# Row maxima and head sums sent round by DMA instead of TensorE transposes, with the order of the DMAs fixed

## The chip, the cores and the metric

The kernel runs on one core of one Trainium2 chip. The metric is the device time of one launch in microseconds (us). In this text PE is TensorE, DVE is VectorE, ACT is ScalarE, POOL is GpSimd, and SP is SyncE, whose queue issues nearly all DMAs of this kernel. SBUF is the on-chip memory of 128 partitions, PSUM the accumulators that TensorE writes (eight banks of 128 x 512 float32).

## The reference

The input x is 4 batches of 2048 rows of 256 float32. Attention with 16 heads of 16, then a normalized residual, then a gated feed-forward whose operands are quantized in blocks of 16 to a 4-bit grid, then a second normalized residual:

```
q, k, v = split_heads(x @ Wq.T), split_heads(x @ Wk.T), split_heads(x @ Wv.T)
attn = softmax(einsum('bhld,bhmd->bhlm', q, k) * SCALE)
x = layernorm(x + merge(einsum('bhlm,bhmd->bhld', attn, v)) @ Wo.T)
x = layernorm(x + fp4_linear(silu(fp4_linear(x, w_gate)) * fp4_linear(x, w_up), w_down))
```

`fp4_linear` scales each block of 16 values by its largest magnitude / 6, rounds to the grid 0, 0.5, 1, 1.5, 2, 3, 4, 6, and multiplies in float32.

## The kernel before

The attention is worked off in 64 steps: 4 batches x 4 blocks of 512 query rows (QB) x 4 groups of 4 heads. A step has 16 periods (NKT), one for each 128 key rows; so the main loop has 1024 periods, and 64 periods make one block of query rows. Periods are counted 0 to 15 within a step below. In a period TensorE makes, by an order written out by hand (ORDER):

- four score products `pm` (line 178, called by `maximum`) of a step ahead: 128 query rows by 512 keys, of which VectorE takes the largest of each row (`mx`, recorded at line 95, the line of the helper class InOrder);
- four score products `pe` (`exponential`) of the present step, turned the other way: 128 keys by 512 query rows, which ScalarE turns into `e` with exp (line 567);
- four products of `e` with the values into the bank `av` (`values`), two periods later. The values carry columns of ones, so that `av` holds each head's numerator and its sum of exponentials, in 16 + 16 rows a head;
- at most one *part* of other work: the projections of a later batch (`square`), the feed-forward (`wide`, `long`) or four transposes (`turn`). A period without a part has the kind `none`.

The maxima run 20 periods (LEAD) ahead of the exponentials. The negative of a row's maximum must stand in the last two of the 64 rows of each head's `q` tile (a high and a low half), opposite rows of ones in `k`, so that the product `pe` is already less the maximum. `max_rows` does that, from period 11 of a step on: VectorE's reduction `nm`, two GpSimd operations that split it into `nh` (lines 537, 538), a part `pn` of four transposes in period 13, a copy `nr` by ScalarE (line 549), and four DMAs from `nr` into the `q` tiles (line 554). The first `pe` that reads them stands in period 0 of the next step of exponentials.

`normalize` divides a finished step, from period 1 of the next step on: ScalarE copies the bank to `av_sb` (line 588), a part `pa` of four transposes turns it in period 3, VectorE takes the reciprocals `rd` of the sums and makes two products `oq`. After every second step a part `pr` of four transposes turns `oq` back, and ScalarE copies it to `oT` (line 615), which the residual's products `py` read.

Work of the feed-forward on VectorE and GpSimd is put into a list of due times (`later`, `take_due`): at most one entry is run in a period, after the last maximum, and none in a period in which `normalize` has set `clock["busy"]`. Quantizing (`fp4`) is such a chain: `amax`, then `sc` and `rs` on VectorE and `xn` on GpSimd, then the mask `m` on VectorE and four GpSimd operations (lines 242 to 245). The generator of the feed-forward goes on only when a number of periods has passed since the last entry.

TensorE's and VectorE's instructions stay in the order of the program (`keep_in_program_order`). Those of ScalarE, GpSimd and the DMAs on SP are placed by a scheduler. SP works in order: a DMA that waits holds all behind it. q, k and v go through DRAM (`qx`, `kx`, `vx`) and are loaded again step by step by `loads`.

Of the kernel before, what the change touches and what calls it, by code (L numbers as in the profile page):

```python
# [35 lines left out]
F32 = mybir.dt.float32  # L36
# [71 lines left out]
def block_kernel(  # L108
# [47 lines left out]
    def later(periods, step, rest=0):  # L156
# [2 lines left out]
        due.append((clock["now"] + periods, step, state))  # L159
        return lambda: state["done"] is not None and clock["now"] >= state["done"] + rest  # L160

    def take_due(most=1):
# [61 lines left out]
    def fp4(pool, t, tag, gain=1.0):  # L224

        p, nb, _ = t.shape
        amax = pool.tile([p, nb], F32, tag="amax" + tag, name="amax")
        vector.tensor_reduce(amax, t, AX.X, ALU.max, apply_absolute_value=True)
        sc = pool.tile([p, nb], F32, tag="sc" + tag, name="sc")
        xn = pool.tile([p, nb, FB], F32, tag="xn" + tag, name="xn", bufs=3 if tag else 2)  # L230

        def scaled():
            vector.tensor_scalar(sc, amax, gain / 6.0, 1e-12, ALU.mult, ALU.max)
            rs = pool.tile([p, nb], F32, tag="rs" + tag, name="rs")
            vector.reciprocal(rs, sc)
            nc.gpsimd.tensor_scalar(rs, rs, gain * TIES_DOWN, 1.0, ALU.mult, ALU.mult)
            nc.gpsimd.tensor_tensor(xn, t, rs.unsqueeze(2).to_broadcast([p, nb, FB]), ALU.mult)
# [9 lines left out]
        later(1, scaled)  # L247
        return xn, later(3, rounded, 4 if tag == "" else 3)

    def fp4_at_once(pool, t, tag, gain=1.0):  # L250

# [36 lines left out]

    kx = [[dram.tile([R, NC, L], F32, tag=f"kx{i}{c}", name=f"kx{i}{c}") for c in range(KC)] for i in range(2)]
    qx = [[dram.tile([R, NC, QB], F32, tag=f"qx{i}{c}", name=f"qx{i}{c}") for c in range(KC)] for i in range(6)]  # L290
    vx = [dram.tile([NG, P, NKT, NP * 3 * DH], F32, tag=f"vx{i}", name=f"vx{i}") for i in range(2)]

    p1 = ctx.enter_context(tc.tile_pool(name="p1", bufs=1))
# [3 lines left out]
    def load_x(b, tb):  # L297

        rows = slice(tb * QB, (tb + 1) * QB)
        if b == 0 and tb >= 2:  # L300
            xb_of[b, tb] = p1.tile([P, QT, D], F32, tag="x1", name="xb", bufs=2)
        else:
            xb_of[b, tb] = p2.tile([P, QT, D], F32, tag="xb", name="xb")
        nc.sync.dma_start(xb_of[b, tb], x[b, rows, :].rearrange("(t p) d -> p t d", p=P))


    loaded = {}
# [40 lines left out]
    def prepare():  # L348
# [82 lines left out]
    def project(b, tb, what):  # L431
# [14 lines left out]
        def q_or_k(name, c):  # L446
# [9 lines left out]
                was_read("pq")  # L456
                yield LEAST

            for i, half in enumerate((hi, lo, hi, lo) if name == "k" else (hi, hi, lo, lo)):
                d = min(DH, RM - i * DH)  # L460
                nc.sync.dma_start(
                    dst[i * DH : i * DH + d].rearrange("r h n -> (r h) n"), half[: d * NC, :].bitcast(F32)
                )
            projected.add((b, tb, name + str(c)))

        def values_of():
            for t in range(QT):
                v = vt[(tb * 2 + t // 2) % 4]
                pv = psum("pv")
                yield product(pv[:, :D], [(xT[:, kc, t * P : (t + 1) * P], wvT[:, kc, :]) for kc in range(KC)])  # L470
                src = pv[:, :D].rearrange("p (g i j d) -> p g i j d", g=NG, i=NP, j=2)
                for j in range(2):
                    nc.scalar.copy(v[:, :, t % 2, :, 2 * j * DH : (2 * j + 1) * DH], src[:, :, :, j, :])
                if t % 2:
                    t0 = tb * QT + t - 1
                    nc.sync.dma_start(
                        vx[b % 2][:, :, t0 : t0 + 2, :].rearrange("g p t c -> p g (t c)"),
                        v.rearrange("p g t i c -> p g (t i c)"),
                    )
                if t == QT - 1:  # L480
                    projected.add((b, tb, "v"))
                was_read("pv")
                yield LEAST

# [6 lines left out]
    def load_q(s):  # L491
        b, qb, g = steps[s]
        for i in range(NP):
            c, h = divmod(g * HG + i * 2, NC)
            q = p1.tile([P, QB], F32R, tag="q", name="q", bufs=3 * NP)
            for j in range(2):
                nc.sync.dma_start(
                    q[R * j : R * j + RM, :].bitcast(F32), qx[(b * NQB + qb) % len(qx)][c][:RM, h + j, :]
                )
            q_sb[s, i] = q  # L500

    def load_k(s, kb):
        b, qb, g = steps[s]
        for i in range(NP):
            c, h = divmod(g * HG + i * 2, NC)
            k = p1.tile([P, QB], F32R, tag="k", name="k", bufs=16)
            for j in range(2):
                nc.sync.dma_start(
                    k[R * j : R * j + R, :].bitcast(F32), kx[b % 2][c][:, h + j, kb * QB : (kb + 1) * QB]
                )  # L510
            k_sb[s, i, kb] = k

    def load_v(s):
        b, qb, g = steps[s]
        assert all((b, tb, "v") in projected for tb in range(NQB))
        v_sb[s] = p1.tile([P, NKT, NP * 3 * DH], F32, tag="v", name="v", bufs=2)
        nc.sync.dma_start(v_sb[s], vx[b % 2][g])

    def maximum(m, h):

        (s, n), (i, j) = divmod(m, NKT), divmod(h, 2)
        if s not in mx_sb:
            mx_sb[s] = p2.tile([P, QT, HG, NQB], F32, tag="mx", name="mx")
# [5 lines left out]
        vector.tensor_reduce(mx_sb[s][:, t, h : h + 1, kb], pm, AX.X, ALU.max)  # L529
        banks_m.append(bank)  # L530

    def max_rows(s):

        nm = p2.tile([P, QT, HG], F32, tag="nm", name="nm")
        vector.tensor_reduce(nm, mx_sb.pop(s), AX.X, ALU.max, negate=True)
        nh = p2.tile([P, QT, HG, 2], F32R, tag="nh", name="nh")
        nc.gpsimd.tensor_scalar(nh[:, :, :, 0], nm, 1.0, 1.0, ALU.mult, ALU.mult)
        nc.gpsimd.tensor_tensor(nh[:, :, :, 1], nm, nh[:, :, :, 0].bitcast(F32), ALU.subtract)
        yield 0
        yield 0  # L540
        pn = psum("pn")
        yield turn(
            [
                (pn[: 2 * HG, t * P : (t + 1) * P], nh[:, t].rearrange("p h c -> p (h c)").bitcast(F32))
                for t in range(QT)
            ]
        )
        nr = p2.tile([2 * HG, QB], F32R, tag="nr", name="nr", bufs=1)
        nc.scalar.copy(nr, pn[: 2 * HG, :])
        was_read("pn")  # L550
        for i in range(NP):
            for j in range(2):
                h = 2 * i + j
                nc.sync.dma_start(
                    q_sb[s, i][R * j + RM : R * j + R, :].bitcast(F32), nr[2 * h : 2 * h + 2, :].bitcast(F32)
                )
        yield LEAST

    def exponential(n, h):

# [19 lines left out]
                stop=(kt == NKT - 1),  # L580
            )

    oTs, oq_of = {}, {}

    def normalize(s):

        av_sb = p2.tile([P, QB], F32, tag="av_sb", name="av_sb", bufs=1)
        nc.scalar.copy(av_sb, av_ps.pop(s))
# [7 lines left out]
        vector.reciprocal(rd, pairs[:, :, :, 1:3, 0])  # L596
        clock["busy"] = True
        if s % 2 == 0:
            oq_of[s // 2] = p2.tile([P, QT, P], F32, tag="oq", name="oq", bufs=1)
# [115 lines left out]
    def feed_forward(b, qb, between):  # L715
        rows = slice(qb * QB, (qb + 1) * QB)
        x1 = p1.tile([P, QT, D], F32, tag="x1", name="x1", bufs=2)
        nc.sync.dma_start(x1, x[b, rows, :].rearrange("(t p) d -> p t d", p=P))
        if between is not None:
            load_x(*between)  # L720
        yield 0
# [24 lines left out]
        def out_rows(t):  # L746
            at = slice(qb * QB + t * P, qb * QB + (t + 2) * P)
            store = out[b, at, :].rearrange("(t p) d -> p t d", p=P)
            layer_norm(x1, t, 2, lambda: nc.sync.dma_start(store, x1[:, t : t + 2, :]))

        yield from gate(0)
        yield from gate(1)
# [218 lines left out]
    def loads(n):  # L971
# [25 lines left out]

    for n in range(-LEAD, N + LAG):
        m = n + LEAD
        loads(n)  # L1000
        if n == N - NKT:
            x1_last = load_last(*steps[-1][:2])
# [34 lines left out]
        if m >= N:  # L1037
            take_due(len(due))
    banks.extend([7])
    while urgent or queue or due or ready:  # L1040
        take_due(len(due))
        whole()
    feed_forward_last(*steps[-1][:2], x1_last)
# [32 lines left out]
```

## Time and profile before

| | us |
|---|---|
| median of 3 runs | 3491.27 (3488.14 to 3494.37) |
| profiled execution, span from the first to the last instruction | 3493.0 |
| TensorE busy | 3395.2 (97%) |
| VectorE busy | 2921.7 (84%) |
| ScalarE busy | 2627.0 (75%) |
| GpSimd busy | 1506.2 (43%) |
| 4096 maxima `mx` on VectorE | 2599.8, 682 ns each |
| transposes `pn`, `pa`, `pr` on TensorE (256, 256, 128) | 38.5, 42.1, 21.0 |
| copies `nr`, `oT` on ScalarE (64, 32) | 36.4, 18.9 |
| `oq`, `rd` on VectorE (128, 64) | 31.3, 15.8 |
| `nh`, two forms, on GpSimd (64 each) | 14.9, 14.3 |

For the profiled execution no time but its span is given, so the span stands for it; the granted TensorE clock has a mean of 0.989 in it. A line of a group reads: line, engine, operation, output <- inputs, shapes, count, then busy time in us and the mean of one in ns, then how long the engine stood idle before it and what ended that. A line of the timeline reads: start and length in us, engine, line, operation, output <- inputs, how many in a row, and in brackets the idle time before it with what ended it. Matmuls overlap each other, so that sums of their durations say little and the distance from one period to the next says more.

### The profile page before, as it was taken

To read this page: it belongs to the slowest core of one execution; us is meant where nothing else is said; L and a number is where in the kernel's file an instruction comes from. 1 tells how busy PE (TensorE), PEld (TensorE's weight loads), DVE (VectorE), ACT (ScalarE), POOL (GpSimd) and SP (SyncE) were. 2 spreads that over 40 slices of the span, in tenths; PEclk is the share of its full clock that TensorE was granted. 3 is DMA by queue.
4 is the path that set the end of the run, shared out by engine and by line. 5 is a ranking of instruction groups with operands and counts; after the bars stand their busy time and mean duration, and the time that the engine had idled before them with its cause. 6 is when DMAs were issued, how large, how long until landed. Compare 5 with 4: busy or idle time off the path is not lost.

```text
span 3493.0 us, 65842 instructions
## 1 busy us (share of the span) xinstructions
PE 3395.2 (97%) x24340; PEld 1798.9 (51%) x24340; DVE 2921.7 (84%) x5130; ACT 2627.0 (75%) x5446; POOL 1506.2 (43%) x1724
## 2 busy tenths in 40 slices
PE   7899999999999999999999999999999999999996
PEld 5444555555555555555555555555554544545444
DVE  5788888888888888888888888888888898888825
ACT  3677777877777787877778777787877778777772
POOL 1243453534435343453535336353443545344361
PEclk9999999999999999999999999999999999999998
DMA  6543323333242332333333242332332122222200
GB/s 208 177 139 114 106 82 120 91 86 108 88 120 76 119 98 63 116 100 109 92 96 102 80 120 88 106 96 76 105 88 82 58 83 69 67 77 76 71 1 12
DMA packets 190678, 328.90 MB, mean 94 GB/s; under 512 B 24344, under 2 KB 68248, under 8 KB 190360
## 3 DMA queue, kind: packets, MB, share of 16 engines
q1 hardware_dynamic: 188968, 323.39, 31.0%
q8 instruction: 195, 3.19, 0.4%
q10 hardware_dynamic: 1392, 1.31, 0.1%
q14 instruction: 123, 1.01, 0.1%
HBM read 237.04 MB, written 86.51 MB: 93 GB/s over the span
## 4 chain that ended last, share of the span: by engine, by line
PE 83%; DVE 10%; POOL 4%; DMA 2%; issue 1%; SPq 0%; ACT 0%; POOLq 0%; ACTq 0%; DVEq 0%
PE av L178 25%; PE pm L178 16%; PE pe L178 16%; DVE mx L95 7%; PE pz L178 6%; PE pg L178 4%; PE pu L178 4%; PE pq L178 3%; PE py L178 2%; PE pth L181 2%; PE pv L178 1%; POOL m L242 1%; PE pn L181 1%; PE pa L181 1%; POOL xn L243 1%; POOL xn L244 1%
## 5 line engine op out<-in xcount | busy, mean ns | idle before, releaser
L95 DVE TENSOR_REDUCE mx<-pm 128x1 f32<-128x512 f32 x4096 | 2599.8, 682 | 414.6 <-PE pm L178 240.6
L567 ACT ACTIVATE e<-pe 128x512 f32<-128x512 f32 x4096 | 2234.7, 602 | 704.3 <-PE pe L178 430.1
L178 PE MATMUL pm<-k,q 62*128 62x512 f32 x4096 | 1631.4, 446 | 45.0 <-DVE mx L95 32.6
L178 PE MATMUL pe<-q,k 64*128 64x512 f32 x4096 | 1555.9, 444 | 0.5 <-ACT read L221 0.3
L178 PE MATMUL av<-e,v 128*32 128x512 f32 x8192 | 1096.4, 607 | 4.5 <-DMA v<-vx 4.5
L178 PEld LDWEIGHTS pm<-k,q 62*128 62x128 f32 x4096 | 720.1, 186 | 721.6 <-DVE mx L95 585.8
L178 PEld LDWEIGHTS pe<-q,k 64*128 64x128 f32 x4096 | 693.6, 185 | 428.9 <-ACT e L567 357.5
L178 PE MATMUL pg<-wgT,xqT 64*128 64x352 f32 (+1 forms) x992 | 351.4, 474 | 1.8 <-ACT xqT L821 1.8
L178 PE MATMUL pu<-wuT,xqT 64*128 64x352 f32 (+1 forms) x992 | 352.5, 473 | 0.0
L178 PEld LDWEIGHTS av<-e,v 128*32 128x32 f32 x8192 | 161.7, 108 | 302.9 <-issue 269.5
L178 PE MATMUL pz<-wdT,hT 64*128 64x128 f32 (+2 forms) x2648 | 312.7, 281 | 1.5 <-ACT hT L858 1.5
L242 POOL TENSOR_SCALAR m<-m 128x704 f32<-128x704 f32 (+2 forms) x100 | 231.8, 2318 | 171.3 <-DVE m L95 169.9
L178 PEld LDWEIGHTS pz<-wdT,hT 64*128 64x128 f32 (+1 forms) x2648 | 299.7, 189 | 8.9 <-ACT hT L858 2.9
L711 POOL TENSOR_TENSOR x<-x,read 128x128 f32<-128x128 f32 x120 | 54.6, 455 | 497.1 <-ACT read L221 496.1
L675 POOL TENSOR_TENSOR a<-a,g 128x352 f32<-128x352 f32 x120 | 112.6, 938 | 344.7 <-ACT a L673 344.6
L683 POOL TENSOR_TENSOR h<-a,u 128x352 f32<-128x352 f32 x120 | 112.5, 937 | 160.7 <-ACT u L681 159.5
L178 PEld LDWEIGHTS pu<-wuT,xqT 64*128 64x128 f32 (+1 forms) x992 | 172.9, 186 | 14.5 <-issue 1.0
L178 PEld LDWEIGHTS pg<-wgT,xqT 64*128 64x128 f32 (+1 forms) x992 | 172.7, 186 | 14.5 <-ACT xqT L821 3.0
L243 POOL TENSOR_TENSOR xn<-xn,m 128x704 f32<-128x704 f32 (+2 forms) x100 | 153.8, 1538 | 6.6
L244 POOL TENSOR_TENSOR xn<-xn,m 128x704 f32<-128x704 f32 (+2 forms) x100 | 153.6, 1536 | 6.1
L245 POOL TENSOR_TENSOR xn<-xn,sc 128x704 f32<-128x704 f32 (+2 forms) x100 | 126.2, 1262 | 7.8
L455 POOL TENSOR_TENSOR klo<-read,khi 128x256 fp32r<-128x256 f32 x64 | 47.7, 747 | 188.2 <-ACT read L221 160.0
(114 smaller groups left out, 2636.5 us busy)
## 6 DMA issues: line engine op xcount, KB each, us to landing
k<-kx SPq DMA_DIRECT2D x1024, 128.0 KB
v<-vx SPq DMA_DIRECT2D x64, 768.0 KB
q<-qx SPq DMA_DIRECT2D x256, 124.0 KB
kx<-khi SPq DMA_DIRECT2D x64, 256.0 KB
qx<-qhi SPq DMA_DIRECT2D x64, 256.0 KB
vx<-vt SPq DMA_DIRECT2D x32, 384.0 KB
xb<-in_L_attn_x_dram SPq DMA_DIRECT2D x16, 512.0 KB
kx<-klo SPq DMA_DIRECT2D x32, 256.0 KB
```

The source lines that it names most:

```text
L95: return lambda *args, **kw: self.tc.keep_in_program_order(getattr(self.engine, name)(*args, **kw))
L178: tc.keep_in_program_order(nc.tensor.matmul(*args, **kw))
L181: tc.keep_in_program_order(nc.tensor.transpose(*args))
L242: nc.gpsimd.tensor_scalar(m, m, 1.0, ROUND, ALU.max, ALU.mult)
L243: nc.gpsimd.tensor_tensor(xn, xn, m, ALU.add)
L244: nc.gpsimd.tensor_tensor(xn, xn, m, ALU.subtract)
L245: nc.gpsimd.tensor_tensor(xn, xn, sc.unsqueeze(2).to_broadcast([p, nb, FB]), ALU.mult)
L455: nc.gpsimd.tensor_tensor(lo[:, cols], read(pq), hi[:, cols].bitcast(F32), ALU.subtract)
L567: nc.scalar.activation(e, pe, AF.Exp, scale=SCALE)
L675: nc.gpsimd.tensor_mul(a, a, g)
L683: nc.gpsimd.tensor_mul(h[:, cols], a, u)
L711: nc.gpsimd.tensor_add(x1[:, t, cols], x1[:, t, cols], read(pz))
```

## The change

The maxima are split by VectorE itself (a copy and a subtraction into `nh`), and one VectorE transpose of 32 x 32 squares makes `nt`. One DMA stores `nt` to a DRAM tile `mr`, and four DMAs load it from there into the rows of the `q` tiles. The part `pn` and the copy `nr` are gone.

In all steps but the last two, `normalize` makes no transposes: two DMAs gather the rows of sums out of `av_sb` into `ends` (128 x 16), three DMAs move the numerators into `num`, VectorE takes the reciprocal `rd`, one DMA stores it to a DRAM tile `sr`, one DMA loads it back, repeated over 16 rows a head, into `den`, and after every second step one GpSimd product of `num` and `den` makes `oT`. The last two steps keep the old way (`normalize_last`).

Within the main loop the DMAs that go through a new helper `dma` (all but those of the weights) stay in the order of the program. Stores of projections, values and output rows are put into the program 2 or 3 periods later than their data (`after`, `send_waiting`). The loads of v move from period 3 to 5 of a step, those of k and q from periods 0, 4, 8, 12 to 1, 5, 9, 13. The preparation of the weights waits until the piece before has been scaled (`taken`).

```diff
+    def dma(out, in_):
+        i = nc.sync.dma_start(out, in_)
+        if pinned["on"]:
+            tc.keep_in_program_order(i)
+
+    def after(periods, send):
+
+        if pinned["on"]:
+            waiting.append((clock["now"] + periods, send))
+        else:
+            send()
...
         for piece, after in zip(pieces, pieces[1:] + [None]):
+            while not q[1].taken():
+                yield LEAST
...
+            after(3, stores)
...
-        nm = p2.tile([P, QT, HG], F32, tag="nm", name="nm")
+        nm = p2.tile([P, HG, QT], F32, tag="nm", name="nm")
         vector.tensor_reduce(nm, mx_sb.pop(s), AX.X, ALU.max, negate=True)
-        nh = p2.tile([P, QT, HG, 2], F32R, tag="nh", name="nh")
-        nc.gpsimd.tensor_scalar(nh[:, :, :, 0], nm, 1.0, 1.0, ALU.mult, ALU.mult)
-        nc.gpsimd.tensor_tensor(nh[:, :, :, 1], nm, nh[:, :, :, 0].bitcast(F32), ALU.subtract)
         yield 0
+        nh = p2.tile([P, HG, 2, QT], F32, tag="nh", name="nh")
+        vector.tensor_copy(nh[:, :, 0, :].bitcast(F32R), nm)
+        vector.tensor_tensor(nh[:, :, 1, :].bitcast(F32R), nm, nh[:, :, 0, :], ALU.subtract)
         yield 0
-        pn = psum("pn")
-        yield turn(
...
-        nr = p2.tile([2 * HG, QB], F32R, tag="nr", name="nr", bufs=1)
-        nc.scalar.copy(nr, pn[: 2 * HG, :])
-        was_read("pn")
+        nt = p2.tile([P, S], F32, tag="nt", name="nt")
+        vector.transpose(nt, nh.rearrange("p h c t -> p (h c t)"))
+        rows = mr[s % 2]
+        dma(rows.rearrange("r (b q) -> b r q", q=S), nt)
+        yield 0
         for i in range(NP):
             for j in range(2):
                 h = 2 * i + j
-                nc.sync.dma_start(
-                    q_sb[s, i][R * j + RM : R * j + R, :].bitcast(F32), nr[2 * h : 2 * h + 2, :].bitcast(F32)
-                )
-        yield LEAST
+                dma(
+                    q_sb[s, i][R * j + RM : R * j + R, :].bitcast(F32),
+                    rows[h * 2 * QT : (h + 1) * 2 * QT].rearrange("(c t) p -> c (t p)", c=2),
+                )
...
     def normalize(s):
+
+        if s >= len(steps) - 2:
+            yield from normalize_last(s)
+            return
+        av_sb = p2.tile([P, QB], F32, tag="av_sb", name="av_sb", bufs=1)
+        nc.scalar.copy(av_sb, av_ps.pop(s))
+        ends = p2.tile([P, QB // S], F32, tag="ends", name="ends")
+        yield 0
+        for i in range(NP):
+            dma(
+                ends[i * R : (i + 1) * R, :],
+                av_sb[i * R + DH : i * R + 3 * DH : DH, :].rearrange("j (c n) -> j c n", n=QB // S),
+            )
...
+        for src, dst, n in ((0, 0, DH), (S + DH, DH, 2 * DH), (3 * S + DH, 3 * DH, DH)):
+            dma(num[at + dst : at + dst + n, :], av_sb[src : src + n, :])
+        for _ in range(3):
+            yield 0
+        rd = p2.tile([P, QB // S], F32, tag="rd", name="rd")
+        vector.reciprocal(rd, ends)
+        clock["busy"] = True
+        yield 0
+        dma(sr[s % 2].rearrange("h (c n) -> (h c) n", n=QB // S), rd)
+        yield 0
+        yield 0
+        dma(den[at : at + R, :], sr[s % 2].unsqueeze(1).to_broadcast([HG, DH, QB]))
+        if s % 2 == 0:
+            return
+        for _ in range(5):
+            yield 0
+        oT = p1.tile([P, QB], F32, tag="oT", name="oT", bufs=3)
+        nc.gpsimd.tensor_tensor(oT, num, den, ALU.mult)
...
-        if kt == 3 and 0 <= n and s + 1 < len(steps):
+        if kt == 5 and 0 <= n and s + 1 < len(steps):
             load_v(s + 1)
-        if n > 0 and kt % QT == 0:
-            ahead, kb = divmod(n - QT + 2 * NKT, NKT)
+        if n > 0 and kt % QT == 1:
+            ahead, kb = divmod(n - 1 - QT + 2 * NKT, NKT)
...
+        pinned["on"] = 0 <= n < N
+        send_waiting()
         loads(n)
```

More of the change, by code (lines that the diff above doesn't have):

```diff
@@ L160, in later, with send_waiting @@
         return lambda: state["done"] is not None and clock["now"] >= state["done"] + rest
+    pinned = {"on": False}
+    waiting = deque()
+    def dma(out, in_):
[7 more added lines that the diff above has]
+            send()
+    def send_waiting(everything=False):
+        for _ in range(len(waiting)):
+            at, send = waiting.popleft()
+            if everything or at <= clock["now"]:
+                send()
+            else:
+                waiting.append((at, send))
     def take_due(most=1):
@@ L290, in block_kernel @@
     qx = [[dram.tile([R, NC, QB], F32, tag=f"qx{i}{c}", name=f"qx{i}{c}") for c in range(KC)] for i in range(6)]
+    mr = [dram.tile([2 * HG * QT, P], F32, tag=f"mr{i}", name=f"mr{i}") for i in range(2)]
+    sr = [dram.tile([HG, QB], F32, tag=f"sr{i}", name=f"sr{i}") for i in range(2)]
     vx = [dram.tile([NG, P, NKT, NP * 3 * DH], F32, tag=f"vx{i}", name=f"vx{i}") for i in range(2)]
@@ L475, in values_of, with store @@
                     t0 = tb * QT + t - 1
[L476 to L481, printed above, removed]
+                    def store(t=t, t0=t0, v=v):
+                        dma(
+                            vx[b % 2][:, :, t0 : t0 + 2, :].rearrange("g p t c -> p g (t c)"),
+                            v.rearrange("p g t i c -> p g (t i c)"),
+                        )
+                        if t == QT - 1:
+                            projected.add((b, tb, "v"))
+                    after(2, store)
                 was_read("pv")
@@ L522, in maximum @@
         if s not in mx_sb:
-            mx_sb[s] = p2.tile([P, QT, HG, NQB], F32, tag="mx", name="mx")
+            mx_sb[s] = p2.tile([P, HG, QT, NQB], F32, tag="mx", name="mx")
         kb, t = n // QT, n % QT
@@ L748, in out_rows @@
             store = out[b, at, :].rearrange("(t p) d -> p t d", p=P)
-            layer_norm(x1, t, 2, lambda: nc.sync.dma_start(store, x1[:, t : t + 2, :]))
+            layer_norm(x1, t, 2, lambda: after(3, lambda: dma(store, x1[:, t : t + 2, :])))
         yield from gate(0)
@@ L1039, in block_kernel @@
     banks.extend([7])
-    while urgent or queue or due or ready:
+    while urgent or queue or due or ready or waiting:
         take_due(len(due))
+        send_waiting(True)
         whole()
```

48 lines of the change are left out of this document (28 added, 20 removed).

## The prediction

> **What bounds the kernel.** I read the page first (busy shares, chain), then the groups, then the timeline and a table by stretch.
>
> ```profile
> PE 3395.2 (97%) x24340; PEld 1798.9 (51%) x24340; DVE 2921.7 (84%) x5130; ACT 2627.0 (75%) x5446; POOL 1506.2 (43%) x1724
> ...
> PE 83%; DVE 10%; POOL 4%; DMA 2%; issue 1%; SPq 0%; ACT 0%; POOLq 0%; ACTq 0%; DVEq 0%
> ```
>
> TensorE carries the chain, but VectorE's maxima are close behind. How close, the periods tell. Each starts four `av` products:
>
> ```profile
> 1758.34 1.07 PE L178 MATMUL av<-e,v 128*32 128x512 f32 x8
> 1761.08 1.07 PE L178 MATMUL av<-e,v 128*32 128x512 f32 x8
> ...
> 1766.24 0.66 PE L181 MATMUL pa<-ident,av_sb 128*128 128x128 f32 x4
> 1767.48 1.07 PE L178 MATMUL av<-e,v 128*32 128x512 f32 x8
> 1769.84 0.66 PE L181 MATMUL pr<-ident,oq 128*128 128x128 f32 x4
> 1771.10 1.07 PE L178 MATMUL av<-e,v 128*32 128x512 f32 x8
> ...
> 1774.02 1.07 PE L178 MATMUL av<-e,v 128*32 128x512 f32 x8
> ```
>
> A period with no part runs in 2.74, one with four transposes in 2.92 to 3.62; over the run, from period start to period start, the pn, pa and pr periods have a mean of 3.25. A period cannot be shorter than VectorE's four maxima, which the chain shows back to back:
>
> ```profile
> 2858.74 2.39 DVE mx L95 x4
> ```
>
> So a freed period ends near 2.45, and then each microsecond of VectorE's side work (quantizing, moments) shows. 64 periods (one query block, 4 steps) repeat:
>
> ```profile
> 1347.30:1554.50 207.20, 205.88 (x1544) 111.08 (x1536) 179.28 (x314) 163.02 (x339) 94.26 (x108) 1.00 0.33 98
> ...
> 2858.70:3063.50 204.80, 201.35 (x1436) 100.92 (x1432) 179.19 (x314) 156.56 (x313) 88.79 (x100) 1.00 0.26 74
> ```
>
> Columns: length, then busy time of PE, weight loads, DVE, ACT, POOL. The second block has 14 parts fewer (no projection of a next batch) and is only 2.4 shorter: a warning of what a freed period is worth. DVE's 179 is the floor of a block.
>
> **The change, part by part.**
>
> *Transposes.* In the main loop the instruction order of the two builds loses 63 pn, 62 pa and 31 pr parts: 156 turn periods become empty ones, 10 a block (14 empty instead of 4). Gross: 10 x (3.25 - 2.45) = 8.0 a block.
>
> *Side work uncovered.* A turn hides some 0.6 of side work, an empty period none. By the changed order the 14 empty periods hold 6.1 of it (moments 0.60, amax 0.88 or 0.68, sc with rs 0.82, m 0.62 or 0.42, and the new operations); the 4 of before held 1.8. Less 4.3: net 3.7 a block.
>
> *A wait that goes.* Once a block VectorE stands before a masking:
>
> ```profile
> 1842.72 0.43 DVE L95 TENSOR_SCALAR m<-xn 128x512 int32<-128x512 int32 x1 [2.07 <-POOL xn L237]
> ```
>
> That period takes 4.40, not 3.13. In the changed order the reciprocal comes two periods ahead of this mask, not one: 3.1 more for POOL. Gain 0 to 1.3; I take 0.9. What is late next is POOL's rounding ahead of the pth parts, three periods after its mask; the first pth reads the other tile, so there is a period in hand.
>
> *VectorE's new operations.* Per step: copy, subtract, 32-column transpose, and rd from SBUF; gone: rd 0.25 and two oq of 0.286, together 0.82. rd stays 0.245 (reciprocal 128x16). The other three have no row. Below: sc of 128x16, 0.153. Above: sc beside a busy POOL, 1.10 (it takes 0.17 alone):
>
> ```profile
> 2861.05 0.17 DVE L95 TENSOR_SCALAR sc<-amax 128x32 f32<-128x32 f32 x1
> 2869.58 1.10 DVE L95 TENSOR_SCALAR sc<-amax 128x32 f32<-128x32 f32 x1
> ```
>
> I take 0.37 for the copy (mean of sc 0.396) and 0.2 for the others: 1.0 a step, in the 6.1 already. At the upper end (1.1 for the copy in each of 64 steps) 47 more; at the lower, 18 less.
>
> *ACT and POOL* lose nr (0.57), half an oT (0.59) and two nh (0.23) a step; POOL gains a 128x512 product in every second step, 1.06 to 1.29 by xn of that size. Both have room (75%, 43%): nothing. But nh behind POOL's rounding stopped TensorE in the start-up:
>
> ```profile
> 509.20 0.22 POOL L538 TENSOR_TENSOR nh<-nm,nh 128x16 fp32r<-128x16 f32 x1
> ...
> 509.48 0.60 PE L181 MATMUL pn<-ident,nh 128*8 128x128 f32 x4 [3.25 <-POOL nh L538]
> ```
>
> That period took 8.0, another 5.4: gain 7 once. The product stands in POOL's order before adds of `read` tiles (two buffers): if den is late, POOL, then ACT's copies, then the banks hold. den needs rd (period 5), one store and one load, some 6, and those adds begin 6 periods later: covered.
>
> *The row maxima's path*, the new wait on TensorE: transpose in period 13 of a step, store to mr, four loads into q's rows, first use in period 16 by pe, with all of TensorE behind it. Four such issues:
>
> ```profile
> 1851.71 2.51 SPq L554 DMA_DIRECT2D q<-nr  x4
> ```
>
> The packets of the first end 1.42 after its issue, those of the last 0.8 after its end. Path: 0.2 + 1.7 (store, a little over that 1.42) + 2.5 + 0.8 = 5.2. Room: from the last maximum of period 12 to that pe, 7.3 to 12.3 before, 8.7 mean; after three empty periods (once a block) 3 x 2.5 less VectorE's lag of 1.4 = 6.1. It fits by 0.9. Upper bound of the store: 4.54, the chain's wait on a 224 KB store to DRAM in the start-up; then the path is 8.0, 1.9 late in the tight step and 0 to 0.5 in others, some 2 to 3 a block, 40 in all. I take 0.6 a block, as the nearest row (4 KB against 16) says it fits.
>
> [...]
>
> *Other DMAs.* A step issues 12 where it issued 4: +500 at 0.35 to 0.6, 175 to 300 on SP, whose 1,965 issues of before take some 900 of 3493, and 17 MB on 329. k and q loads move one period later and still lead their use by 7 periods (22), v loads two, with 13 in hand. ends has three periods (7.5 or more) for 0.6 of copy, 1.2 of issues and 1.5 to land: covered, unless SP stands at something ahead; behind rd wait all maxima. In program order a store of lo or of output rows waits on SP 2 or 3 periods after its data was asked for, with the loads behind it: covered by those 7 periods. The weights' loads are not pinned; the two stops at them (4.4 and 3.9 on VectorE) stay.
>
> **Sum.** Block: -3.7 - 0.9 + 0.6 = -4.0. Sixteen blocks: -64, with start-up -7: -71. I give back 0.8 a block (13) for bumps where empty periods meet VectorE waiting on POOL, as the second block above shows (periods of 3.7 and 4.0 among 2.7): -58. The profiled execution's span is 3493.0 and the median of the runs 3491.3, so what lies around the span is within the runs' spread: 3493 - 58 = 3435.
>
> **The rivals.**
> - *A freed period is worth little* (0.15). By the block without projections, 2.4 / 14 = 0.17 each; 156 x 0.17 = 27: 3466. Against it: those periods took over quantizing and a POOL stop of 2; the new ones mostly do not.
> - *DRAM's round trip stops TensorE* (0.13), the slower side. Decides once the path exceeds the room by 1.1 in all 62 steps (65 us), that is some 9 long: a store of 4.5 and the loads behind k's four issues (2.4). At 10: 62 x 2 = 124 - 58: 3559. For it: a queue that waits in order. Against: the issues and landing above.
> - *Empty periods run ahead* (0.10). VectorE enters each row of empty periods up to a period ahead (2.23 and 2.33 for two that hold 0.6); two more rows a block than before, 1 each: -32 more, 3403.
> - *Not as said*: the order shows the transposes gone; none.
>
> **Numbers.** Forecast 0.62, 3410 to 3460. The range takes in the first and third rival and the copy's upper end: 3393 to 3487. Faster 0.83, the same (within 0.2%, 7 us, about what a measurement can tell) 0.03, slower 0.14.
>
> **What would show it.** A block of 203 (not 207.2); 14 empty periods in it of 2.4 to 3.3; pn and pr gone, pa in the last two steps only; no 2.07 before m; PEld pm waiting more on DVE mx. Wrong: TensorE waiting on DMA q<-mr at a step's start, DVE on ends, POOL's oT on den with ACT behind it, or a copy near 1.1.

## The result, and the profile after

The changed kernel takes **3621.12 us** in the median of four runs (3613.83 to 3627.0); the kernel before, run beside it, 3490.93 (3488.14 to 3494.37). The ratio is 1.037 (95% interval 1.0355 to 1.0385): **slower by 130 us**, where 3435 was forecast and 3487 was the top of the range. The profiled execution has a span of 3612.1 us and a mean granted TensorE clock of 0.969 (0.989 before).

From the page of the changed kernel, the busy times and the chain by engine:

```profile
PE 3375.5 (93%) x23712; PEld 1789.5 (50%) x23712; DVE 2927.1 (81%) x5198; ACT 2577.8 (71%) x5351; POOL 1517.2 (42%) x1627
...
PE 70%; DVE 14%; DMA 9%; POOL 3%; issue 2%; SPq 1%; ACT 1%; POOLq 0%; ACTq 0%; DVEq 0%
```

628 TensorE instructions are gone and no other engine has much more to do, yet TensorE's share falls from 97 to 93% and 9% of the chain is DMA (2% before). Something waits that did not wait. The table by stretch says where: the first line is one block of 64 periods (207.20 before), the others are parts of it. Columns: length, busy time of PE, weight loads, DVE, ACT, POOL, then the granted clock, the DMA engines' share and GB/s.

```profile
1820.60:2034.20 213.60, 203.46 (x1498) 109.88 (x1498) 178.56 (x317) 159.68 (x333) 95.39 (x102) 0.98 0.33 101
...
1842.50:1848.50 6.00, 6.00 (x72) 4.54 (x66) 4.46 (x7) 3.96 (x9) 0.00 (x0) 1.00 0.14 52
...
1850.00:1856.60 6.60, 0.51 (x6) 0.18 (x3) 0.69 (x1) 0.32 (x2) 2.02 (x3) 0.85 0.39 99
1856.60:1860.60 4.00, 4.00 (x23) 3.18 (x27) 1.19 (x2) 2.41 (x6) 0.62 (x3) 0.50 0.00 0
```

From 1850.0 to 1856.6 TensorE is busy for 0.51 of 6.60 us and the other engines little more (GpSimd most, 2.02), and for the next 4 us TensorE runs at half its clock. Counted in periods from the block's start, this is period 9 (a `pz` part), and there is a second, shorter stop in period 41 (`pu`): over ten steady blocks their medians are 10.12 and 6.80 us, where the kernel before took 3.55 and 3.52. Otherwise the block is much as forecast; its 14 empty periods take between 2.3 and 3.8 us.

What stops it is read from the timelines of the engines in that stretch, taken together:

```profile
1832.55 1.74 SPq L166 DMA_DIRECT2D q<-qx  x4
1834.39 5.61 SPq L166 DMA_DIRECT2D k<-kx  x4
1840.10 0.54 SPq L166 DMA_DIRECT2D sr<-rd  x1
1849.40 0.59 SPq L166 DMA_DIRECT2D den<-sr  x1
...
1854.58 1.26 POOL L652 TENSOR_TENSOR oT<-num,den 128x512 f32<-128x512 f32 x1 [23.02 <-DMA k<-kx]
1855.80 1.28 POOL L783 TENSOR_TENSOR x<-x,read 128x128 f32<-128x128 f32 x3
...
1856.28 0.27 ACT L244 COPY read<-pz 128x128 f32<-128x128 f32 x1 [7.68 <-POOL x L783]
...
1856.60 0.79 PE L201 MATMUL pe<-q,k 64*128 64x512 f32 x1 [6.10 <-ACT read L244]
```

Read it from the bottom. TensorE waits 6.10 us for a copy of ScalarE. ScalarE has waited 7.68 for a `read` tile that GpSimd's adds must free. Those adds stand behind the product `oT` in GpSimd's order, and GpSimd has been idle for 23.02. The profile puts that wait down to a load of k that landed about then, in 16 of 31 cases; in 11 others it names `den`, which the product reads. Its load was issued at 1849.40, and not sooner because SP waited for the store `sr`, issued at 1840.10. In period 41 the chain names both transfers:

```profile
1945.29 8.42 DMA sr<-rd
1953.73 4.36 DMA den<-sr
1958.12 0.08 issue
1958.21 1.26 POOL oT L652
1959.47 0.89 POOL h L755
```

The store of 8 KB takes 7.8 to 9.7 us from its issue to the end of its last packet in the steps of the ten steady blocks, while the other new round trip, that of the maxima, is quick (SP's waits: in total, times, longest):

```profile
SPq L166 <- DMA sr<-rd: 333.2, 62, 9.0
...
SPq L166 <- DMA mr<-nt: 70.2, 63, 1.5
```

By the packet records of the trace, 112 of the store's 128 packets of 64 bytes have ended 1.76 us after its issue (median of 62), the last 16 only at 8.64. Sixteen of 128 is the share of two engines in sixteen. And while they are late (1842.5 to 1848.5 in the table above) the DMA engines are busy to 0.14 of sixteen, that is 2.2 of them, with packets of 2048 bytes. Packets of that size belong to the four loads of q, issued just ahead with 62 rows each, and to the four of k behind them, with 64.

For four loads of k alone, with 64 rows each and packets of the same size, the changed kernel has another figure: a share of 0.70 at 205 GB/s (1879.50 to 1881.50), that is 11.2 engines. That the loads of q, with 62 rows, run on two engines is my estimate from the 0.14 and the 16 late packets; the trace does not show what sets the number of engines. Whether the loads of q are really the cause is what the experiments had to show.

The kernel before had these loads too, and its chain had shown their price in the start-up:

```profile
17.69 4.54 DMA qx<-qlo
23.30 12.26 DMA q<-qx
```

My prediction used the first of these two lines as its upper bound of a store, and not the second.

### The profile page after: what moved, and what is told of

It reads as the page before. It is cut to its first block, busy times and chain, and to the rows that moved or that the text cites. A ratio compares the mean times of both kernels' runs of the same rounds, so it can differ in the third digit from the quotient of the medians.

```text
span 3612.1 us, 65349 instructions
## 1 busy us (share of the span) xinstructions
PE 3375.5 (93%) x23712; PEld 1789.5 (50%) x23712; DVE 2927.1 (81%) x5198; ACT 2577.8 (71%) x5351; POOL 1517.2 (42%) x1627
## 4 chain that ended last, share of the span: by engine, by line
PE 70%; DVE 14%; DMA 9%; POOL 3%; issue 2%; SPq 1%; ACT 1%; POOLq 0%; ACTq 0%; DVEq 0%
PE av L201 22%; PE pe L201 15%; PE pm L201 15%; DVE mx L95 10%; PE pz L201 4%; DMA sr<-rd 4%; PE pq L201 3%; PE pu L201 3%; PE pg L201 3%; DMA k<-kx 2%; DMA den<-sr 2%; PE pth L204 2%; PE pv L201 2%; PE py L201 1%; POOL oT L652 1%
## 5 line engine op out<-in xcount | busy, mean ns | idle before, releaser
L201 PE MATMUL pm<-k,q 62*128 62x512 f32 x4096 | 1668.6, 458 | 76.6 <-DVE mx L95 57.9
L201 PE MATMUL pe<-q,k 64*128 64x512 f32 x4096 | 1590.3, 450 | 112.6 <-ACT read L244 74.1
L201 PEld LDWEIGHTS pm<-k,q 62*128 62x128 f32 x4096 | 733.9, 188 | 703.6 <-DVE mx L95 587.8
L201 PEld LDWEIGHTS pe<-q,k 64*128 64x128 f32 x4096 | 706.4, 188 | 646.3 <-ACT e L596 447.8
L201 PE MATMUL pz<-wdT,hT 64*128 64x128 f32 (+2 forms) x2648 | 321.5, 289 | 1.5 <-ACT hT L930 1.5
L201 PEld LDWEIGHTS pz<-wdT,hT 64*128 64x128 f32 (+1 forms) x2648 | 308.1, 197 | 7.7 <-ACT hT L930 2.9
L652 POOL TENSOR_TENSOR oT<-num,den 128x512 f32<-128x512 f32 x31 | 39.2, 1263 | 544.1 <-DMA k<-kx 268.8
```

Source lines behind the costliest of these rows:

```text
L201: tc.keep_in_program_order(nc.tensor.matmul(*args, **kw))
L652: nc.gpsimd.tensor_tensor(oT, num, den, ALU.mult)
```

## The experiments

The theory after the result: the loss is the product `oT`, which stands early in GpSimd's order and waits for `den`, late behind the loads of q. Rivals: (1) the pinned order of the DMAs or the later loads, (2) the maxima's way through DRAM and VectorE's new work, (3) freed periods are worth little anyway.

### The product pinned later: e_pin

```diff
-        nc.gpsimd.tensor_tensor(oT, num, den, ALU.mult)
+        tc.keep_in_program_order(nc.gpsimd.tensor_tensor(oT, num, den, ALU.mult))
```

> The changed kernel, with one thing more: GpSimd's product oT is pinned to the place in GpSimd's order where the program writes it (five periods after the load of den is issued), behind the residual adds, which the scheduler had put after it. Theory: the loss is that early place. GpSimd waits there for den, behind it the adds of the `read` tiles, ScalarE's copies and then TensorE, twice in each block of 64 periods. Then the two stops go (10.95 us in period 9 of a block and 6.15 in period 41 become 3.3 to 3.6 each, some 10.2 a block, 163 in all, and what the lowered clock behind each stop cost comes on top): 3435 to 3465. Rival 1, the pinned order of the DMAs and the later loads of q and k are what is late: nothing of it changes here, 3600 or more. Rival 2, the maxima's way through DRAM and the new work on VectorE: also unchanged, 3600 or more. Rival 3, the freed periods of TensorE are worth little: the stops go but the time ends near the kernel before, 3475 to 3495.

Measured: 3549.65 us, ratio to the kernel before 1.0165 (1.015 to 1.018). None of the expectations. The stops in periods 9 and 41 are gone (3.21 and 3.51), so their cause is where the theory put it; but period 12 now takes 9.27 instead of 3.32, and TensorE waits 74.7 us in all for `oT` in 14 blocks. The kernel with both edits, e_both below, shows why.

### The loads of q cut: e_qsplit, and both: e_both

```diff
-                dma(
-                    q[R * j : R * j + RM, :].bitcast(F32), qx[(b * NQB + qb) % len(qx)][c][:RM, h + j, :]
-                )
+                for lo, hi in ((0, 32), (32, RM)):
+                    dma(
+                        q[R * j + lo : R * j + hi, :].bitcast(F32),
+                        qx[(b * NQB + qb) % len(qx)][c][lo:hi, h + j, :],
+                    )
```

> The changed kernel, its product oT left in its early place on GpSimd, but each load of q's 62 rows cut into one of 32 rows and one of 30 rows, so that the store of the reciprocals (sr) does not stand behind 248 packets on two of the sixteen DMA engines. Theory: the store sr then lands some 2 us after its issue (8.7 now), den is issued and lands some 6.5 us sooner, GpSimd waits some 6.5 us less for it, and TensorE's stops of 7.4 and 2.8 us fall to under 1: 3440 to 3475. If the lateness of den comes from something else (the number of transfers in SP's order, the round trip through DRAM as such), the store lands as late as before and the time stays at 3600 or more.

Measured: **3422.33 us**, ratio 0.9799 (0.9785 to 0.9814): with the same transfers cut in two the change is a gain of 2%. Lines of its timelines (SP, GpSimd), of its waits and of its table by stretch (a steady block) answer those above:

```profile
1740.47 0.53 SPq L166 DMA_DIRECT2D sr<-rd  x1
1744.02 0.58 SPq L166 DMA_DIRECT2D den<-sr  x1
...
1748.25 1.27 POOL L654 TENSOR_TENSOR oT<-num,den 128x512 f32<-128x512 f32 x1 [5.74 <-DMA k<-kx]
```

```profile
SPq L166 <- DMA sr<-rd: 90.2, 51, 3.2
```

```profile
1733.00:1935.70 202.70, 200.06 (x1498) 108.22 (x1498) 179.56 (x317) 159.51 (x333) 95.19 (x102) 1.00 0.36 106
```

The store's last packet ends 1.61 us after its issue (8.64 before the cut) and `den` is issued 3.6 after the store in these lines, not 9.3. The product still stands early in GpSimd's order and still waits; it is done before ScalarE runs out of `read` tiles. In period 9 its place is not quite the same: in this build one of the four `read` adds stands ahead of it, in the changed kernel none. That this is not the cure is shown by e_q64 below, where all four stand behind it. The clock of the block is 1.00 again. It went below the expected 3440 because a steady block gains 11.8 where I had counted 10.2, and because the first period begins 12 us sooner, which I had left out.

> Both edits: oT pinned where the program writes it, and the loads of q cut into 32 and 30 rows. Theory: each of them takes away the same stop, so the two together give little more than either alone: 3430 to 3460, within 15 of the pinned one. If the two causes were separate, the gains would add: the sum of both single gains.

Measured: 3526.99, ratio 1.0099 (1.0084 to 1.0114): a miss. The cut takes 23 us off the pinned kernel, which is what it takes off at the start-up (first period 12.8 us sooner, first two blocks 11.5 less); the stop of period 12 stays. The store is quick here too (1.61), so it is not den that the product waits for, as the timelines of GpSimd, VectorE and TensorE show:

```profile
1806.72 0.18 DVE L95 BATCH_NORM_AGGREGATE mv<-st 128x2 f32<-128x6 f32 x1
...
1807.00 0.22 POOL L706 TENSOR_SCALAR rstd<-mv 128x2 f32<-128x2 f32 x1 [9.01 <-DVE nt L95]
1807.30 0.19 POOL L709 TENSOR_SCALAR minus<-mv 128x2 f32<-128x2 f32 x1
1807.46 0.71 POOL L707 TENSOR_TENSOR rstd<-rstd,minus_half 128x2 f32<-128x2 f32 x1
1808.28 1.09 POOL L711 TENSOR_SCALAR x<-x,minus,rstd 128x256 f32<-128x256 f32 x2
1809.34 1.26 POOL L654 TENSOR_TENSOR oT<-num,den 128x512 f32<-128x512 f32 x1
...
1810.65 0.79 PE L201 MATMUL py<-woT,oT 64*128 64x256 f32 x1 [5.34 <-POOL oT L654]
```

Pinned to where the program writes it, the product falls behind a layer norm for which VectorE's moments come at 1806.72, and `py`, which reads `oT`, waits 5.34. So the early place is the better one. The fault was the lateness of den, not the place.

### How much of it: e_qquarter

```diff
-                for lo, hi in ((0, 32), (32, RM)):
+                for lo, hi in ((0, 32), (32, RM)) if i == j == 0 else ((0, RM),):
```

The line is that of the cut kernel: here only the first of a step's four loads is cut.

> The changed kernel with only the first of the four loads of q cut into 32 and 30 rows: a smaller dose of the same medicine. Theory: 93 instead of 124 packets of 0.1 us are left on each of the two DMA engines, so the store lands some 3.1 us sooner; the stop in period 9 falls from 7.4 to about 4.3 us over its usual time and the one in period 41 (2.8 over) goes: 16 x 5.9 = 94, and some 3 at the start-up, so 3505 to 3545. If a threshold decides instead (the store is late or it is not), it is either near 3422 or unchanged at 3600 or more.

Measured: 3553.04, ratio 1.018 (1.0155 to 1.0205), 8 above the expected band. The stops shrink together (medians 8.51 in period 9, 4.94 in period 41), so it is graded and no threshold. I had the dose too large: the store's last packet comes 1.1 us sooner (7.56), not 3.1.

### Another queue for the store: e_sr_act

```diff
-        dma(sr[s % 2].rearrange("h (c n) -> (h c) n", n=QB // S), rd)
+        tc.keep_in_program_order(nc.scalar.dma_start(sr[s % 2].rearrange("h (c n) -> (h c) n", n=QB // S), rd))
```

> The changed kernel, loads of q whole, with the store of the reciprocals (sr) alone issued from ScalarE's queue instead of SP's. Theory, if the store is late because it stands in one queue behind the packets of q: in a queue of its own it lands in 2 to 3 us, the stops in periods 9 and 41 of a block go, 3440 to 3475 (a little of it lost where ScalarE issues the store). Rival, the two DMA engines are full whatever the queue: the store lands 8 to 9 us after its issue as now, 3600 to 3635.

Measured: 3620.74, ratio 1.0371 (1.0355 to 1.0386): no gain, but not for the rival's reason alone. The store lands after 4.65 us instead of 8.64: a queue of its own helps, though a part of the difference is that half of these stores are issued later. In the steady blocks those that are issued 6.1 to 7.0 us after the first load of q take 5.0 to 5.7; on SP's queue they are issued 7.3 to 9.6 us after it and take 7.8 to 9.7. The later ones, 9.4 and over 15 us after it, take 4.2 to 4.5 and 2.9 to 3.0. Period 41 is back at its usual length (3.51; there the product also stands one `h` later in GpSimd's order, and this run does not show which of the two did it), period 9 is half cured (6.54), and period 22 now takes 9.90. There ScalarE stands at the issue of the store with its exponentials behind it (timeline of ScalarE; `rd` had been ready since 1913.2):

```profile
1915.29 0.41 ACT L244 COPY read<-pq 128x256 f32<-128x256 f32 x1
1921.93 0.33 ACTq L643 DMA_DIRECT2D sr<-rd  x1
1922.30 2.08 ACT L596 ACTIVATE e<-pe 128x512 f32<-128x512 f32 x4 [6.60 <-DMA k<-kx]
```

SP's four issues of kx at that moment are 2.5 us apart (1913.86 to 1921.54); why an issue from ScalarE is held up with them, no run here shows.

### The parts of the change: e_max, e_before_qsplit, e_max_qsplit

The maxima's path alone (the old normalization in every step, the rest of the change kept):

```diff
-        if s >= len(steps) - 2:
+        if True:
             yield from normalize_last(s)
             return
```

> The changed kernel with the normalization of the kernel before for all steps (two sets of TensorE transposes, VectorE's products), so that only the new path of the maxima, the pinned DMA order and the later loads are left of the change. Theory: with no product on GpSimd there is no stop. Four of a block's ten freed periods remain (4 x 0.8 = 3.2), with the wait of m that went (0.9), less about 1.2 of uncovered side work and readback: some 2 to 3 a block, 16 blocks, and the 7 of the start-up: 3435 to 3460. Rival 1 (pinned DMA order, later loads) and rival 2 (maxima through DRAM, VectorE's new work): they are all still here, so 3600 or more. Rival 3, freed periods worth little: 3475 to 3495.

Measured: 3473.09, ratio 0.9944 (0.9928 to 0.9961). There is no stop: rivals 1 and 2 fall. The time is 13 above the theory's band and next to rival 3's, but a block takes 205.1, 2.1 less than before, as the theory has it; the miss is in the first two blocks, which take 16 more than those of the kernel before (443.0 and 426.6), where I had counted a gain of 7.

The control, the kernel before with its loads of q cut:

```diff
-                nc.sync.dma_start(
-                    q[R * j : R * j + RM, :].bitcast(F32), qx[(b * NQB + qb) % len(qx)][c][:RM, h + j, :]
-                )
+                for lo, hi in ((0, 32), (32, RM)):
+                    nc.sync.dma_start(
+                        q[R * j + lo : R * j + hi, :].bitcast(F32),
+                        qx[(b * NQB + qb) % len(qx)][c][lo:hi, h + j, :],
+                    )
```

> The kernel before, with only its loads of q cut into 32 and 30 rows: the control for the split. Theory: the kernel before has no store of reciprocals and no product on GpSimd that waits behind those loads, so only the start-up gains, where the first maxima wait for q (the changed kernel began its first period 12 us sooner with the split): 3474 to 3484, and a block of 64 periods stays at 207.2. Rival: the loads of 62 rows cost the kernel before in every block too, and the fast time of the split kernel is the split's and not the change's: 3440 or less, blocks of 204 or less.

Measured: 3469.03, ratio 0.9938 (0.9923 to 0.9952), 5 below the band. A steady block stays at 207.2: nothing there waited for what stood behind those loads. The start-up gains 10 up to the first period and 10 in the first two blocks.

The maxima's path with the cut (`if True:` as in e_max, and the loads of e_qsplit):

> The changed path of the maxima, the old normalization everywhere, and the loads of q cut into 32 and 30 rows. Together with the same without the cut (3473.09) and with the whole change with the cut (3422.33) it shares the gain out between the two parts. Theory: the cut gives only the start-up here (12): 3458 to 3466, a block stays at 205.0, and the normalization without transposes is worth the other 35 to 45 (2.3 a block). Rival, the cut helps the maxima's path as well: 3445 or less.

Measured: 3450.59, ratio 0.9882 (0.9867 to 0.9897), 7 below the band; the cut gives 22 here, as it does on the kernel before, and the block stays at 205.0. All with the cut, then: 3469.03 before, 3450.59 with the maxima's path, 3422.33 with the whole change. The maxima's path is worth 18, the normalization 28, the whole **47 us**.

### The pinned order: e_pinlate, e_nopin, e_nopin_whole

Each is one line; the first two have the cut, the third has the loads whole.

```diff
-        pinned["on"] = 0 <= n < N
+        pinned["on"] = 4 * NKT <= n < N   # e_pinlate
+        pinned["on"] = False              # e_nopin and e_nopin_whole
```

> The changed kernel with the loads of q cut, and SP's order of the DMAs left to the scheduler for the first 64 periods; pinned from period 64 on. With the cut alone, the first block takes 224.8 us where the kernel before with the same cut takes 205.4; three of its periods (30, 52 and 56) take 9.9, 9.0 and 6.8 us. Theory: the pinned order makes that: an x load that TensorE's transposes wait for stands behind SP's wait for the maxima's store, and v and q behind a weight load that waits for GpSimd. Then the first block falls to 205 to 215 and the time to 3404 to 3415. Rival, the later loads of q and k or the round trips of the maxima make it: the first block stays above 220, 3418 to 3428.

Measured: 3416.47, ratio 0.9785 (0.9771 to 0.98). The first block takes 219.0, so the theory holds for a part only: period 30, where an x load had stood behind SP's wait for the maxima's store, falls from 9.9 to 3.1; periods 52 and 56 (9.1 and 6.75) stay.

> The changed kernel with the loads of q cut, and no DMA pinned at all: SP's order is the scheduler's everywhere, and no store or load is put off. Theory: the pinned order is worth little in the steady blocks (which the cut alone brought to 202.7), since the waits of SP for the round trips through DRAM are short now: 200 to 207 a block, 3400 to 3440. Rival, pinning carries the changed kernel, and without it the round trips' waits put k and v loads late: 208 or more a block, 3490 or more.

Measured: 3418.74, ratio 0.9792 (0.9775 to 0.9808), steady blocks 202.7. With the cut, pinning makes no difference that these runs can tell.

> The changed kernel with its loads of q whole (62 rows) and no DMA pinned. Rival 1, the pinned order itself makes the store late and the stops: without it they go and the time is that of the unpinned kernel with the cut, 3418.74, and 10 to 12 for the start-up: 3425 to 3440. Theory, the 62-row loads make it: they are still ahead of the store in SP's order (the scheduler puts them some 4 to 5 us earlier than the pinned program does), so the store still lands 3 to 6 us after its issue and a part of the stops stays: 3470 to 3570.

Measured: 3552.55, ratio 1.0159 (1.0131 to 1.0188): in the theory's band, but by another road. The stops in 9 and 41 are gone and the store is on time (2.87 us): the scheduler issues the loads of q earlier. Now another small transfer stands behind them, `ends`, as the chain shows, and VectorE waits for it before the reciprocal (its timeline):

```profile
1853.75 11.84 DMA ends<-av_sb
```

```profile
1865.69 0.25 DVE L95 RECIPROCAL rd<-ends 128x16 f32<-128x16 f32 x1 [2.24 <-DMA ends<-av_sb]
```

A load of 4 KB takes 11.84 us. A block takes 208.8. So the order picks which small transfer is caught behind the loads, and with it how much is lost (3552.55 against 3621.12), but with these loads whole there is a loss either way, and with them cut there is none either way; rival 1 falls.

### No cut, but 64 rows: e_q64

```diff
-                    q[R * j : R * j + RM, :].bitcast(F32), qx[(b * NQB + qb) % len(qx)][c][:RM, h + j, :]
+                    q[R * j : R * j + R, :].bitcast(F32), qx[(b * NQB + qb) % len(qx)][c][:, h + j, :]
```

Beside it, twelve small stores at the start fill the two new rows in DRAM with ones, and the pinning begins at period 64.

> Another cure without more loads: each load of q takes all 64 rows of its tile in DRAM (the last two, filled once at the start with ones, are overwritten by the maxima's rows as before), and the DMA order is pinned from period 64 on, as in the run that was best so far (3416.47). Theory: what matters is only that the row count divides among the sixteen engines, so this does the same as the cut with half as many loads for SP: the store lands in 1.5 to 3 us and the time is 3408 to 3422. If instead the smaller loads made the gain, the stops come back: 3500 or more.

Measured: 3419.29, ratio 0.9785 (0.9768 to 0.9803); the store lands in 1.78 us and a block takes 202.7. The cure is neither smaller nor more loads: 64 rows in one load do it, 62 do not. That the row count has to divide among the engines, as the expectation has it, is not shown: 64, 62 and 32 with 30 are all the counts that were run. Nor is it the place of the product, which here stands ahead of all four `read` adds of the `pz` parts, as in the changed kernel (timeline of GpSimd):

```profile
1745.27 1.28 POOL L657 TENSOR_TENSOR oT<-num,den 128x512 f32<-128x512 f32 x1 [13.51 <-DMA den<-sr]
1746.51 0.87 POOL L788 TENSOR_TENSOR x<-x,read 128x128 f32<-128x128 f32 x2
```

At the start the twelve stores stand in the way (first period at 90.0, against 80.9).

All kernels side by side, from the traces (medians over ten steady blocks; "store" is from its issue to the end of its last packet; time in us):

```
kernel            q rows   store   period 9  period 12  period 41   block   first period at   time
before              62       -       3.55      3.12       3.52      207.2        92.5        3491
e_before_qsplit   32+30      -       3.55      3.12       3.51      207.2        82.3        3469.03
changed             62      8.64    10.12      3.32       6.80      214.5        93.9        3621.12
e_qquarter       1 of 4 cut 7.56     8.51      3.33       4.94      210.6        88.5        3553.04
e_sr_act            62      4.65     6.54      3.33       3.51      215.9        92.4        3620.74
e_nopin_whole       62      2.87     3.21      3.33       3.51      208.8        93.6        3552.55
e_pin               62      8.68     3.21      9.27       3.51      210.1        93.8        3549.65
e_both            32+30     1.61     3.21      9.27       3.51      210.3        81.0        3526.99
e_max               62       -       3.03      3.13       3.12      205.1        93.5        3473.09
e_max_qsplit      32+30      -       3.01      3.12       3.13      205.0        81.6        3450.59
e_qsplit          32+30     1.61     3.21      3.33       3.51      202.7        81.8        3422.33
e_nopin           32+30     1.61     3.21      3.33       3.51      202.7        81.8        3418.74
e_q64               64      1.78     3.21      3.33       3.51      202.7        90.0        3419.29
e_pinlate         32+30     1.65     3.21      3.33       3.51      202.7        80.9        3416.47
```

e_pinlate, e_nopin, e_q64 and e_qsplit lie within 6 us and are all 2% ahead of the kernel before; 22 us of that any of them shares with the old kernel when its loads are cut.

## Why the prediction was wrong

**The step that failed** is one that was costed at nothing: "den needs rd (period 5), one store and one load, some 6, and those adds begin 6 periods later: covered." Three things are in it.
- The store and the load, from the store's issue to the product, took 14.5 in period 9 (1840.10 to 1854.58) and 12.9 in period 41, not 6. This term decides: with the cut the two take 7.8 in period 9, and nothing stops.
- "6 periods later" was wrong as well. It fits the kernel before, where a steady block has `rd` in period 3 and these adds (of the `pz` parts, L711 there) from 9 on. In the changed order `rd` stands in period 5, and with the cut the adds run in periods 7 to 10, two to five after it.
- The consequence, "POOL, then ACT's copies, then the banks hold", was right word for word. The hazard was named, the row that prices it stood in the trace of before (12.26 us for the loads of q), and I priced the small transfer as if it were alone. I asked of each transfer how long it takes, and not what is ahead of it on the same engines.

**What a stop costs** is more than its idle time: TensorE waits 74.1 us for copies of `read` and 36.3 for `a` (14 times each), 7.9 a block; the two periods together are 10.2 longer than with the cut, and the block 11.8. The rest lies in the periods right behind them, 10 (1.1 longer) and 42 (0.5). At least a part of the difference is the clock behind a stop: 0.50 for 4 us in the stretch shown, where a `pe` product takes 0.79 instead of 0.50.

**The other steps**, read with the cut against the kernel before with the cut, so that the failed one is out:
- *Steady block*: the sum gave -4.0 + 0.8 = -3.2, that is 204.0; "a block of 203 (not 207.2)" is the -4.0 alone. Measured 202.7: -4.4 (207.16 to 202.74), of which the maxima's path -2.1. The 0.8 given back for bumps did not come.
- *VectorE's new operations*: 1.0 a step. In the changed kernel the copy has a mean of 0.221, the subtract 0.442, the transpose 0.193, rd 0.241: 1.10. The sum was right, the parts were not; the subtract and not the copy is the slow one.
- *The wait of m on xn* is gone from that period (26 of a block): it took 4.21 and takes 2.57, a gain of 1.6 where 0.9 was taken.
- *The row maxima's path*: it fits. TensorE waited once for q<-mr, 1.9 us. The four issues take 0.25 each, not 0.6. From the issue of the store `mr` to the issue of the first load behind it 2.02 pass (median of 64), where I had 1.7 for the store.
- *Start-up*: the gain of 7 came. The two periods that it was read from, 61 of the first and of the second block, fall from 5.7 and 8.5 to 2.7 and 3.2. But the first two blocks together went from 416.2 to 422.4, where 2 x -3.2 - 7 = -13.4 was forecast: 20 that the sum does not have at all. 15.6 of them are three periods of the first block: 30, 52 and 56 take 9.9, 9.0 and 6.75, and 3.1, 3.1 and 3.85 in the kernel before with the cut. Period 30 is the x load behind SP's wait for the maxima's store, a consequence of pinning (e_pinlate). In periods 52 and 56 the chain of e_qsplit passes through a weight load and GpSimd, but no run isolates them.
- *SP's issues*, off the path: 502 more, as forecast, but they take 347 us more, not 175 to 300, and those of the kernel before took 1,117 in all, not 900.

Together: -47 measured against -58 forecast, the start-up's 20 being more than the whole difference. The dismissed hazard is the other 177 (3621 - 3422, less the 22 that the cut gives the kernel before as well): -47 + 177 = +130, the measured loss.

**The rivals.** "DRAM's round trip stops TensorE" (3559) had the right mechanism at the wrong transfer: the maxima's store is not behind the loads of q, the reciprocals' is. "A freed period is worth little" and "empty periods run ahead" are both out: the gain in steady blocks lies between them.

## What to carry to other kernels

Before a small transfer goes on the path, list what is issued just before it and on how many DMA engines that runs; here a store of 8 KB took 8.64 us behind loads of 62 rows, and 1.61 to 1.78 behind the same data in 32 and 30 or in 64 rows. When a new instruction waits for such a transfer, look in the built order, not in the program, for what stands behind it on its in-order engine, and count buffers from there. A cure may only move the fault (to `py` in e_pin, to `ends` in e_nopin_whole, to ScalarE in e_sr_act): look at every period again, not only at the one that was mended.

## What the runs showed of the hardware

- From 1842.5 to 1848.5, with the loads of q under way (four, of 62 rows of 2048 bytes each), the sixteen DMA engines had a share of 0.14, about two of them (52 GB/s); with four loads of k, of 64 such rows each, it was 0.70 (205 GB/s, 1879.50 to 1881.50). Of the 128 packets of the store that was issued behind the loads of q, 112 had ended 1.76 us after its issue and the last 16 only at 8.64 (medians); behind loads of 32 and 30 rows the last ended at 1.61 (e_qsplit).
- With the store issued from ScalarE's queue that wait was shorter and not gone: 5.0 to 5.7 us when it was issued 6.1 to 7.0 us after the first load of q, against 7.8 to 9.7 from SP's queue, 7.3 to 9.6 us after it.
- After TensorE had been idle for 6.1 us the granted clock was 0.50 for the next 4 us and 0.90 in the 4.4 after that. At which length of idleness the clock falls, this stretch does not show.
